# An adaLN transformer block on one core: when the inner rows' weights, the last operands, the slices' sums and the modulation weights are loaded and made

## Chip, core, metric

One core of a Trainium2 chip; everything is fp32. The metric is the device time of one execution in microseconds (us). A core has TensorE (PE, with its weight loads as PEld), VectorE (DVE), ScalarE (ACT), GpSimd (POOL) and SyncE (SP), whose queue issues nearly all DMAs of this kernel, in order.

## What is computed

For two sequences of 1024 tokens with D = 1024, one block with modulation from a vector c (six vectors per sequence: shift, scale and gate, for attention and for the FFN):

```
mod = silu(c) @ Wmod                      # sa, ca, ga, sf, cf, gf; |ga|, |gf| at least 0.25
h   = layernorm(x) * (1 + ca) + sa
q, k, v = clip(h @ Wqkv.T, -8, 8)         # q and k: layer norm over D, then 32 heads of 32
p   = softmax(q k^T / sqrt(32) + ALiBi + causal mask)
x1  = x + ga * ((p v) @ Wout.T)
h2  = layernorm(x1) * (1 + cf) + sf
x2  = x1 + gf * (ad * ((silu(ag * (h2 @ Wg.T)) * (au * (h2 @ Wu.T))) @ Wd.T))   # inner size 2752
```

## The kernel before

**Products.** Every large product is done in the Strassen-Winograd form with seven half-block products instead of eight (`seven`; the products are called P1, P2, U2, P5, U3, P53, U6). Its operands are sums and differences of quarters. For weights these sums are made on the chip and stored to device memory: `out_weights` for Wout, `down_weights` for Wd. `down_weights` works in 20 slices of 512 rows by two times 128 columns; a slice is four loads (L1211), four POOL subtractions (L1212 to L1215) and, a step later, four stores (L1218), in a pool with two buffers (tile `wdr`).

**Stages.** First come the modulation vectors, of which a first part is done ahead and the rest (`mod_product`, L618) is spread between the projection's products by `late`; `AHEAD` says how many loads (tile `wm`, pool `wmr`) run ahead of them. Then `projections` makes q, k, v of batch 0 and then of batch 1 (parts q, k, v by blocks of 256 tokens). From v of batch 0 on, attention runs beside it: `together` interleaves two generators, `attention` and `dense_work`, by `share`, which says how many us of dense work go with so many of attention. `dense_work` is the rest of batch 0's projection, batch 1's projection with the slices of `down_weights` as `side` work, and then `output` (Wout, gate, residual, second layer norm, turning rows) for the four blocks of batch 0 and the first two of batch 1.

`attention` goes by groups (batch, half of the queries, four heads) and by key blocks of 128: `scores` (products, exp on ACT at L1084, on the diagonal a causal mask by POOL's affine_select, L1088), `weigh` (product with V, and the sums of p for the softmax by DVE and POOL, L1116), `settle` (sums across partitions, stored; after the last head group of a half, `reciprocals` stores 1/sum as `rec`). A group's q, k and v (`chunk`: cq, ck, cv) are loaded when the second group before it ends.

`operand(b, j)` makes the seven operands of an output block: four loads of `rb` (the reciprocals spread over partitions, L1246), four of `ao` (L1260), four muls (L1261), four sums (L1262 to L1266); A21 and A22 have two buffers. `output` loads x (`xr`, L1289), reads the banks (L1293 to L1305), stores x1 (L1310) and puts layer norm and turning on a list.

After attention come the inner rows: 2752 is 5 x 512 + 192, and the last 192 rows of Wg and Wu are done apart by `rest_rows` with three weight tiles `restw`, made by `rest_weights` (a memset on POOL, L1365, and four loads, L1370). They are interleaved with the last two output blocks (1,2) and (1,3) and with the making of the FFN's operands (`second_batch`). `h2` of finished blocks is fetched again (tiles `hl`). Then comes the FFN.

**Order.** From the start of attention PE's order is the order in which the program writes its instructions. The order on the other engines is a scheduler's, within the data dependencies and explicit ties (`behind(a, b)`: a not before b). A pool that is opened where another has been closed takes its memory, and its tiles wait for the last users there.

What follows attention before the change:

```python
fetch(0, 0, nc.scalar)
rest_w = rest_weights(rest_pool, nc.scalar)     # loads on ACT's queue
fetch(1, 0, nc.scalar)
made = {(1, NJ // 2): operand(1, NJ // 2, opools[1])}
fetch(0, 1)
with_turns(rows((0, 0), (1, 0)))
fetch(1, 1)
...                                             # between(): rows (0, 1), second(0), rows (1, 1)
together(between(), output(1, range(NJ // 2, NJ), *out_args, made, 3), lambda a: 0.6 * OUT_US / 2 * a / 20.6)
```

Of the kernel before, what the change touches and what calls it, by code (L numbers as in the profile page):

```python
# [12 lines left out]
FP = mybir.dt.float32  # L13
# [5 lines left out]
P = 128  # L19
# [461 lines left out]
def kernel(  # L481
# [19 lines left out]
    nc = tc.nc  # L501
# [49 lines left out]
    NJ = NT // 2  # L551
# [111 lines left out]
    with tc.tile_pool(name="prep", bufs=1) as prep, tc.tile_pool(  # L663
        name="wmod", bufs=2 * KC
# [43 lines left out]
    def behind(ins, first):  # L708

        tc.add_manual_dep(  # L710
            ins.ins, first.ins.name,
            mybir.DependencyInfo(mybir.DependencyClass.NoSync, mybir.DependencyReason.DATA),
            reason="behind",
        )

    last_exp = [None]

    def normalize(tiles, outs, small, nm):

# [308 lines left out]
    def attention(pools, adders, banks):  # L1028
# [22 lines left out]
        def scores(b, qb, k, jb):  # L1051
            qc, kc, _ = chunks[b, qb, k]
            y0 = max(qb * QB, jb * P)
            end = (qb + 1) * QB
            n = end - y0
            span = SPAN.get(k, QB)
            out_ = {}
            first = None

            for half in (1, 0):  # L1060
                sp = scp.tile([P, 2, QB], FP, tag=f"sc{half}", name=f"sc_{b}_{k}_{qb}_{jb}_{half}")
                p = prp.tile(
                    [P, 2, QB], FP, tag="p" if jb else f"p0{half}", name=f"p_{b}_{k}_{qb}_{jb}_{half}",
                    bufs=None if jb else 2,
                )
                for g in range(2):
                    r0 = (2 * half + g) * HD
                    ins = matmul(
                        sp[:, g, 0:n], kc[r0 : r0 + HD, ts(jb, P)], qc[r0 : r0 + HD, ds(y0 - qb * QB, n)],
                        start=True, stop=True,  # L1070
                    )
                    if first is None:
                        first = ins
                    else:
                        behind(ins, first)
                out_[half] = (sp, p)
            for half in range(2):
                sp, p = out_[half]
                for g in range(2):
                    h_ = 4 * k + 2 * half + g  # L1080
                    for y in range(y0 // span * span, end, span):
                        lo, hi = max(y, y0) - y0, y + span - y0
                        d = jb - y // P + {128: 7, 256: 6, 512: 4}[span]
                        last_exp[0] = nc.scalar.activation(  # L1084
                            p[:, g, lo:hi], sp[:, g, lo:hi], AF.Exp, bias=kw[:, d, h_ : h_ + 1]
                        )
                if jb * P >= qb * QB:
                    nc.gpsimd.affine_select(  # L1088
                        out=p[:, :, 0:P], in_=p[:, :, 0:P], pattern=[[0, 2], [1, P]],
                        compare_op=ALU.is_ge, fill=0.0, base=0, channel_multiplier=-1,  # L1090
                    )
            return [out_[half][1] for half in range(2)]
# [110 lines left out]
    def down_weights(i, pool):  # L1203


        s, c_ = i // 4, i % 4
        w = pool.tile([P, 5, 2, P], FP, tag="wdr", name=f"wdr_{i}")
        rows_ = wd_t[ds(s * 4 * P, 4 * P), :].rearrange("(j p) e -> p j e", p=P)
        for kh in range(2):
            for n in range(2):  # L1210
                nc.sync.dma_start(w[:, 2 * kh + n], rows_[:, 2 * kh : 2 * kh + 2, ds(n * HALF + c_ * P, P)])  # L1211
        nc.gpsimd.tensor_sub(w[:, 0], w[:, 1], w[:, 0])  # L1212
        nc.gpsimd.tensor_sub(w[:, 4], w[:, 3], w[:, 0])
        nc.gpsimd.tensor_sub(w[:, 1], w[:, 3], w[:, 1])
        nc.gpsimd.tensor_sub(w[:, 2], w[:, 2], w[:, 4])  # L1215
        yield
        for o, r in (("T1", 0), ("T2", 4), ("T3", 1), ("T4", 2)):
            nc.sync.dma_start(wd_dram[o][:, s, :, ts(c_, P)], w[:, r])  # L1218
        yield
# [18 lines left out]
        rows_ = wd_t[0 : NSB * 4 * P, :].rearrange("(s m l p) e -> m l p s e", m=2, l=2, p=P)  # L1238
        return rows_[kh, l][:, :, ds(n * HALF + c * 256, 256)]

    def operand(b, j, ap_):

        qb, y0 = 2 * j * P // QB, 2 * j * P % QB
        rb = ap_.tile([P, KC, 2 * P], FP, tag="rb", name=f"rb_{b}_{j}")
        for g in range(4):
            nc.sync.dma_start(  # L1246
                rb[ts(g, HD)],
                rec_dram[b][qb].rearrange("(k g) q -> g k q", g=4)[g][:, ds(y0, 2 * P)].partition_broadcast(HD),
            )
        a = {  # L1250
            q: ap_.tile(
                [P, KC // 2, P], FP, tag=q, name=f"ao{q}_{b}_{j}",
                bufs=2 if q in ("A21", "A22") else None,
            )
            for q in ("A11", "A12", "A21", "A22", "S1", "S2", "S4")
        }
        for m, kh, q, eng in (
            (0, 0, "A11", nc.vector), (0, 1, "A12", nc.gpsimd), (1, 1, "A22", nc.vector), (1, 0, "A21", nc.gpsimd),
        ):
            nc.sync.dma_start(a[q], ao_dram[b][qb][:, ds(kh * 4, 4), ds(y0 + m * P, P)])  # L1260
            eng.tensor_mul(a[q], a[q], rb[:, ds(kh * 4, 4), ts(m, P)])  # L1261
        nc.vector.tensor_add(a["S1"], a["A21"], a["A22"])  # L1262
        nc.vector.tensor_sub(a["S2"], a["S1"], a["A11"])
        a["S3"] = a["A21"]
        nc.gpsimd.tensor_sub(a["S3"], a["A11"], a["A21"])
        nc.gpsimd.tensor_sub(a["S4"], a["A12"], a["S2"])  # L1266
        return a
# [3 lines left out]
    def output(b, js, pools, banks, bt, todo, keep, made={}, q0=1):  # L1271
# [9 lines left out]
        for j in js:  # L1281
# [9 lines left out]
            part_t = {}  # L1291

            def read(q, bank):  # L1293
                if q in ("P1", "U2", "P5"):
                    part_t[q] = partp.tile([P, 512], FP, tag=q, name=f"o{q}_{b}_{j}")
                    nc.scalar.copy(part_t[q], bank)
                    return
                m, n = QUAD[q]
                yg = partp.tile([P, 512], FP, tag=f"yg{n}", name=f"yg_{q}_{b}_{j}")
                if q == "U6":  # L1300
                    nc.vector.tensor_mul(yg, ga[:, ts(n, HALF)], bank)
                else:
                    nc.vector.tensor_add(yg, part_t[MATE[q]], bank)
                    nc.gpsimd.tensor_mul(yg, yg, ga[:, ts(n, HALF)])
                nc.gpsimd.tensor_add(xs[m][:, ts(n, HALF)], xs[m][:, ts(n, HALF)], yg)  # L1305

# [114 lines left out]
    three = [bankp.tile([P, 512], FP, tag=f"bank{i}", name=f"bank{i}") for i in range(3)]  # L1421
    with ExitStack() as st:
        five = st.enter_context(tc.tile_pool(name="five", bufs=1, space=PSUM))
        wmr = st.enter_context(tc.tile_pool(name="wmr", bufs=4))
        mrw = st.enter_context(tc.tile_pool(name="mrw", bufs=1))
        wosp = st.enter_context(tc.tile_pool(name="wos", bufs=1))
        nxp = st.enter_context(tc.tile_pool(name="next", bufs=1))
# [4 lines left out]
        banks = Banks(three[0:2], three[2:3] + more[2:5])  # L1432
        sums = {g: more[g - 1] for g in range(1, NMOD // 2)}
        pieces = [(g, k, n0) for k in range(KC) for g in sums for n0 in (0, 2)]
        AHEAD = 3
        loaded = []
        left = list(range(len(pieces)))

# [57 lines left out]
    def dense_work():  # L1496
        yield from dense0
        with tc.tile_pool(name="wdsum", bufs=2) as dwp:
            steps = itertools.chain.from_iterable(down_weights(i, dwp) for i in range(4 * NSB))

            def side(n, e):

                at = 7 * n + e - 24
                if at >= 0 and at % 3 != 2:
                    next(steps, None)

            yield from projections(1, qpools, banks, 1, side=side)
            for _ in steps:
                pass
        early.close()  # L1510
        hbp = right["hb"] = ost.enter_context(tc.tile_pool(name="hb", bufs=1))
        wop = ost.enter_context(tc.tile_pool(name="wo", bufs=1))
        gap_, tkp, partp, osm, aop = [
            ost.enter_context(tc.tile_pool(name=n, bufs=k))
            for n, k in (("oga", 1), ("tok", 4), ("opart", 1), ("osmall", 2), ("ao", 1))
        ]
        opools = (gap_, aop, tkp, partp, hbp, osm)
        made = {(0, 0): operand(0, 0, opools[1])}
        bt = weights_b(wop, wout_t, "o", wt_dram[3])
        out_args.extend((opools, banks, bt, Todo(banks), keep))  # L1520
        yield from output(0, range(NJ), *out_args, made)
        yield from output(1, range(NJ // 2), *out_args)


# [13 lines left out]
    pair_st = ctx.enter_context(ExitStack())  # L1538
    rest_st = ctx.enter_context(ExitStack())
    pair_pool = right["rest"] = pair_st.enter_context(tc.tile_pool(name="pair", bufs=1, side="right"))  # L1540
    rest_pool = rest_st.enter_context(tc.tile_pool(name="rest", bufs=1, side="right"))
    rps = rest_st.enter_context(tc.tile_pool(name="rest_ps", bufs=4, space=PSUM))

# [15 lines left out]
        together(rows_, todo.run(len(todo.list), True), lambda a: 0.16 * (a - 9.0))  # L1559

    fetch(0, 0, nc.scalar)
    rest_w = rest_weights(rest_pool, nc.scalar)
    fetch(1, 0, nc.scalar)
    made = {(1, NJ // 2): operand(1, NJ // 2, opools[1])}
    fetch(0, 1)
    with_turns(rows((0, 0), (1, 0)))
    fetch(1, 1)
# [477 lines left out]
```

## Time and profile before

| | |
|---|---|
| time, median of 3 runs | 2912.99 us (2908.82 to 2913.18) |
| the profiled execution: time, span | 2906.93 us, 2905.2 us |
| busy: PE, DVE, POOL, ACT | 2723.2, 1448.4, 1294.0, 685.7 us |
| mean granted PE clock | 0.976 |
| DMA | 579 MB, mean 199 GB/s |
| batch 0's projection alone | to about 350 us |
| attention beside dense work | to 1394 us |
| inner rows and the last two output blocks | 1394 to about 1557 us |
| FFN | from there to the end |

The profile is one execution, the times of its rows are on its own scale. PE is busy for 94% of the span, so what can be read from it are the stretches in which PE is empty or its granted clock (PEclk, a share of full speed) is under 1, and what ended each wait. In a window's row come its bounds, its length, and then the busy time of each engine with the number of instructions; in a wait's row the waiting engine, tile and line, then what it waited for, the us in total, the number of times and the longest; in a group's row the busy us and mean ns of one, and then the idle time of the engine just before them.

### The profile page before, as it was taken

The numbers are of one execution on the slowest core, as the hardware profiler recorded it, in microseconds if no ns is written. First come the engines' busy times: TensorE is split into PE (matmuls) and PEld (weight loads), VectorE is DVE, ScalarE is ACT, GpSimd is POOL, SyncE is SP. The second block draws the span as 40 slices with busy tenths as digits, with TensorE's granted clock in tenths as the row PEclk, the third lists the DMA queues.
The fourth block names the chain that finished last, engine by engine and source line by source line (L and its number), as shares of the span: only waits on it lengthen the run. The fifth ranks groups of instructions, "written<-read, shape, count | busy, mean of one in ns | idle before, by whom it ended". The sixth has DMA issues, their size and how long they took to land. (4 is left out here: it accounts for less than half of the span.)

```text
span 2905.2 us, 29905 instructions
## 1 busy us (share of the span) xinstructions
PE 2723.2 (94%) x10271; PEld 1336.5 (46%) x10271; DVE 1448.4 (50%) x2285; ACT 685.7 (24%) x1523; POOL 1294.0 (45%) x1270
## 2 busy tenths in 40 slices
PE   6999898999999898988799999999999998999998
PEld 2444333333333232222565444444444446888776
DVE  5765522566643456666464353453535346444442
ACT  1322232344444456555021011010101100000000
POOL 3311146523454665656357455464744541222343
PEclk9999999999999899999899999999999999999999
DMA  9877797563461555432777667585766659555542
GB/s 341 301 254 282 295 312 223 174 217 114 173 178 62 210 171 150 147 107 86 222 234 252 217 213 244 169 278 167 263 199 195 233 165 289 158 152 145 157 145 81
DMA packets 377573, 579.14 MB, mean 199 GB/s; under 512 B 21590, under 2 KB 278712, under 8 KB 366276
## 3 DMA queue, kind: packets, MB, share of 16 engines
q1 hardware_dynamic: 359768, 554.54, 58.8%
q10 hardware_dynamic: 17644, 22.59, 2.5%
q8 instruction: 84, 1.38, 0.2%
q14 instruction: 77, 0.63, 0.1%
HBM read 411.89 MB, written 165.17 MB: 199 GB/s over the span
## 5 line engine op out<-in xcount | busy, mean ns | idle before, releaser
L1084 ACT ACTIVATE p<-sc,kw 128x128 f32<-128x128 f32 (+3 forms) x1024 | 421.7, 513 | 382.5 <-PE sc L762 365.4
L762 PE MATMUL bank<-wT,a 128*128 128x512 f32 x768 | 360.0, 612 | 14.0 <-DVE raw L983 7.1
L1116 POOL TENSOR_TENSOR p<-p,p 128x1024 f32<-128x1024 f32 (+3 forms) x128 | 259.3, 2026 | 243.6 <-PE av L762 211.5
L1116 DVE TENSOR_TENSOR p<-p,p 128x1024 f32<-128x1024 f32 (+3 forms) x192 | 243.8, 1280 | 190.4 <-POOL p L1088 132.8
L762 PE MATMUL bank<-wB,a 128*128 128x512 f32 x576 | 266.0, 606 | 2.1 <-DVE raw L981 1.3
L762 PE MATMUL sc<-cq,ck 32*128 32x512 f32 (+3 forms) x1536 | 193.5, 543 | 53.0 <-ACT p L1084 52.7
L762 PEld LDWEIGHTS bank<-wT,a 128*128 128x128 f32 x768 | 142.6, 195 | 192.7 <-issue 174.6
L1088 POOL TENSOR_SCALAR_AFFINE_SELECT p<-p 128x256 f32<-128x256 f32 x256 | 139.2, 560 | 125.9 <-ACT p L1084 123.3
L762 PE MATMUL av<-p,cv 128*32 128x512 f32 (+3 forms) x1536 | 173.9, 514 | 16.6 <-POOL p L1088 16.6
L762 PEld LDWEIGHTS bank<-wB,a 128*128 128x128 f32 x576 | 105.1, 191 | 149.5 <-issue 128.8
L762 PEld LDWEIGHTS sc<-cq,ck 32*128 32x128 f32 x1536 | 64.9, 187 | 190.3 <-ACT p L1084 101.6
L1817 PE MATMUL gy<-bt,sig 128*128 128x512 f32 x280 | 132.5, 596 | 10.8 <-DMA bt<-bop_B 6.2
L1817 PE MATMUL gx<-bt,sig 128*128 128x512 f32 x280 | 131.6, 592 | 0.0
L1817 PE MATMUL uy<-bt,siu 128*128 128x512 f32 x280 | 131.6, 592 | 0.0
L1817 PE MATMUL ux<-bt,siu 128*128 128x512 f32 x280 | 131.6, 592 | 0.0
L762 PEld LDWEIGHTS av<-p,cv 128*32 128x32 f32 x1536 | 34.4, 110 | 139.1 <-issue 85.3
L1817 PEld LDWEIGHTS gy<-bt,sig 128*128 128x128 f32 x280 | 52.4, 190 | 81.1 <-issue 71.5
L1817 PEld LDWEIGHTS ux<-bt,siu 128*128 128x128 f32 x280 | 53.2, 190 | 66.9 <-issue 64.3
L1817 PEld LDWEIGHTS gx<-bt,sig 128*128 128x128 f32 x280 | 53.2, 190 | 66.9 <-issue 66.6
L1817 PEld LDWEIGHTS uy<-bt,siu 128*128 128x128 f32 x280 | 53.2, 190 | 66.9 <-issue 66.2
L762 PE MATMUL rest<-hl,restw 128*128 128x256 f32 x288 | 67.7, 394 | 15.7 <-DMA x<-xr 15.7
L1817 PE MATMUL gx<-bt,wgS 128*128 128x512 f32 x160 | 75.2, 592 | 0.0
(416 smaller groups left out, 4481.2 us busy)
## 6 DMA issues: line engine op xcount, KB each, us to landing
bt<-bop_T SPq DMA_DIRECT2D x140, 512.0 KB
bt<-bop_B SPq DMA_DIRECT2D x99, 512.0 KB
a<-hop SPq DMA_DIRECT2D x20, 1792.0 KB
wm<-in_L_wmod_dram SPq DMA_DIRECT2D x48, 512.0 KB
wB<-in_L_attn_Wqkv_dram SPq DMA_DIRECT2D x21, 1024.0 KB
aq_S<-act_S SPq DMA_DIRECT2D x16, 1280.0 KB
qk<-qs SPq DMA_DIRECT2D x16, 1024.0 KB
act_S<-asS SPq DMA_DIRECT2D x30, 512.0 KB
```

The costliest lines, as they stand in the source:

```text
L762: return in_order(nc.tensor.matmul(*args, **kw_))
L1084: last_exp[0] = nc.scalar.activation(p[:, g, lo:hi], sp[:, g, lo:hi], AF.Exp, bias=kw[:, d, h_ : h_ + 1])
L1088: nc.gpsimd.affine_select(out=p[:, :, 0:P], in_=p[:, :, 0:P], pattern=[[0, 2], [1, P]], compare_op=ALU.is_ge, fill=0.0, base=0, channel_mu ...
L1116: adders[b](half, jb).tensor_add(dst, dst, ps[half][:, :, 0:n])
L1817: nc.tensor.matmul(ps.rearrange("p (j t) -> p j t", j=NJ), ins[mat][qa][:, c2, :], bt[:, :, c2, :], start=(q in ("P1", "P2", "P5") and c2 ...
```

## The change

- `down_weights` has three steps instead of two: loads; sums; stores. The first sum of a slice is tied behind the last causal mask written so far (`last_mask`). `side` takes a step at each of its calls from call 24 on, where it took two of three; 20 slices are 60 steps where they were 40.
- The inner rows' weights get a pool of their own (`restw`) beside the output stage's pools, and are loaded on SP's queue after the output blocks of batch 0 are written, instead of on ACT's queue after attention.
- Operands (1,2) and (1,3) are both made right after attention, ahead of the inner rows; (1,2) has its own pool `wide`. In `operand`, A22 has one buffer instead of two.
- In `output`, the gated values `yg` are written over P's copies (U6 over P5's) instead of into tiles of their own; x rows have three buffers instead of four, the layer norm's small tiles one instead of two.
- The modulation weights have six buffers instead of four and run five ahead of their products instead of three.

```diff
@@ -714,6 +714,7 @@
         )
 
     last_exp = [None]
+    last_mask = [None]
 
     def normalize(tiles, outs, small, nm):
 
@@ -1085,7 +1086,7 @@
                             p[:, g, lo:hi], sp[:, g, lo:hi], AF.Exp, bias=kw[:, d, h_ : h_ + 1]
                         )
                 if jb * P >= qb * QB:
-                    nc.gpsimd.affine_select(
+                    last_mask[0] = nc.gpsimd.affine_select(
                         out=p[:, :, 0:P], in_=p[:, :, 0:P], pattern=[[0, 2], [1, P]],
                         compare_op=ALU.is_ge, fill=0.0, base=0, channel_multiplier=-1,
                     )
@@ -1203,13 +1204,15 @@
     def down_weights(i, pool):
 
 
+
         s, c_ = i // 4, i % 4
         w = pool.tile([P, 5, 2, P], FP, tag="wdr", name=f"wdr_{i}")
         rows_ = wd_t[ds(s * 4 * P, 4 * P), :].rearrange("(j p) e -> p j e", p=P)
         for kh in range(2):
             for n in range(2):
                 nc.sync.dma_start(w[:, 2 * kh + n], rows_[:, 2 * kh : 2 * kh + 2, ds(n * HALF + c_ * P, P)])
-        nc.gpsimd.tensor_sub(w[:, 0], w[:, 1], w[:, 0])
+        yield
+        behind(nc.gpsimd.tensor_sub(w[:, 0], w[:, 1], w[:, 0]), last_mask[0])
         nc.gpsimd.tensor_sub(w[:, 4], w[:, 3], w[:, 0])
         nc.gpsimd.tensor_sub(w[:, 1], w[:, 3], w[:, 1])
         nc.gpsimd.tensor_sub(w[:, 2], w[:, 2], w[:, 4])
@@ -1238,7 +1241,7 @@
         rows_ = wd_t[0 : NSB * 4 * P, :].rearrange("(s m l p) e -> m l p s e", m=2, l=2, p=P)
         return rows_[kh, l][:, :, ds(n * HALF + c * 256, 256)]
 
-    def operand(b, j, ap_):
+    def operand(b, j, ap_, own=None):
 
         qb, y0 = 2 * j * P // QB, 2 * j * P % QB
         rb = ap_.tile([P, KC, 2 * P], FP, tag="rb", name=f"rb_{b}_{j}")
@@ -1248,9 +1251,9 @@
                 rec_dram[b][qb].rearrange("(k g) q -> g k q", g=4)[g][:, ds(y0, 2 * P)].partition_broadcast(HD),
             )
         a = {
-            q: ap_.tile(
+            q: (ap_ if q == "S4" or own is None else own).tile(
                 [P, KC // 2, P], FP, tag=q, name=f"ao{q}_{b}_{j}",
-                bufs=2 if q in ("A21", "A22") else None,
+                bufs=2 if q == "A21" and own is None else None,
             )
             for q in ("A11", "A12", "A21", "A22", "S1", "S2", "S4")
         }
@@ -1296,11 +1299,12 @@
                     nc.scalar.copy(part_t[q], bank)
                     return
                 m, n = QUAD[q]
-                yg = partp.tile([P, 512], FP, tag=f"yg{n}", name=f"yg_{q}_{b}_{j}")
+
+                yg = part_t[MATE.get(q, "P5")]
                 if q == "U6":
                     nc.vector.tensor_mul(yg, ga[:, ts(n, HALF)], bank)
                 else:
-                    nc.vector.tensor_add(yg, part_t[MATE[q]], bank)
+                    nc.vector.tensor_add(yg, yg, bank)
                     nc.gpsimd.tensor_mul(yg, yg, ga[:, ts(n, HALF)])
                 nc.gpsimd.tensor_add(xs[m][:, ts(n, HALF)], xs[m][:, ts(n, HALF)], yg)
 
@@ -1421,7 +1425,7 @@
     three = [bankp.tile([P, 512], FP, tag=f"bank{i}", name=f"bank{i}") for i in range(3)]
     with ExitStack() as st:
         five = st.enter_context(tc.tile_pool(name="five", bufs=1, space=PSUM))
-        wmr = st.enter_context(tc.tile_pool(name="wmr", bufs=4))
+        wmr = st.enter_context(tc.tile_pool(name="wmr", bufs=6))
         mrw = st.enter_context(tc.tile_pool(name="mrw", bufs=1))
         wosp = st.enter_context(tc.tile_pool(name="wos", bufs=1))
         nxp = st.enter_context(tc.tile_pool(name="next", bufs=1))
@@ -1432,7 +1436,7 @@
         banks = Banks(three[0:2], three[2:3] + more[2:5])
         sums = {g: more[g - 1] for g in range(1, NMOD // 2)}
         pieces = [(g, k, n0) for k in range(KC) for g in sums for n0 in (0, 2)]
-        AHEAD = 3
+        AHEAD = 5
         loaded = []
         left = list(range(len(pieces)))
 
@@ -1500,8 +1504,7 @@
 
             def side(n, e):
 
-                at = 7 * n + e - 24
-                if at >= 0 and at % 3 != 2:
+                if 7 * n + e >= 24:
                     next(steps, None)
 
             yield from projections(1, qpools, banks, 1, side=side)
@@ -1512,13 +1515,15 @@
         wop = ost.enter_context(tc.tile_pool(name="wo", bufs=1))
         gap_, tkp, partp, osm, aop = [
             ost.enter_context(tc.tile_pool(name=n, bufs=k))
-            for n, k in (("oga", 1), ("tok", 4), ("opart", 1), ("osmall", 2), ("ao", 1))
+            for n, k in (("oga", 1), ("tok", 3), ("opart", 1), ("osmall", 1), ("ao", 1))
         ]
         opools = (gap_, aop, tkp, partp, hbp, osm)
         made = {(0, 0): operand(0, 0, opools[1])}
         bt = weights_b(wop, wout_t, "o", wt_dram[3])
+        rwp = ost.enter_context(tc.tile_pool(name="restw", bufs=1))
         out_args.extend((opools, banks, bt, Todo(banks), keep))
         yield from output(0, range(NJ), *out_args, made)
+        right["w"] = rest_weights(rwp, nc.sync)
         yield from output(1, range(NJ // 2), *out_args)
 
 
@@ -1538,6 +1543,7 @@
     pair_st = ctx.enter_context(ExitStack())
     rest_st = ctx.enter_context(ExitStack())
     pair_pool = right["rest"] = pair_st.enter_context(tc.tile_pool(name="pair", bufs=1, side="right"))
+    wide = rest_st.enter_context(tc.tile_pool(name="wide", bufs=1, side="right"))
     rest_pool = rest_st.enter_context(tc.tile_pool(name="rest", bufs=1, side="right"))
     rps = rest_st.enter_context(tc.tile_pool(name="rest_ps", bufs=4, space=PSUM))
 
@@ -1559,9 +1565,10 @@
         together(rows_, todo.run(len(todo.list), True), lambda a: 0.16 * (a - 9.0))
 
     fetch(0, 0, nc.scalar)
-    rest_w = rest_weights(rest_pool, nc.scalar)
+    rest_w = right["w"]
     fetch(1, 0, nc.scalar)
-    made = {(1, NJ // 2): operand(1, NJ // 2, opools[1])}
+    made = {(1, NJ // 2): operand(1, NJ // 2, opools[1], wide)}
+    made[1, NJ // 2 + 1] = operand(1, NJ // 2 + 1, opools[1])
     fetch(0, 1)
     with_turns(rows((0, 0), (1, 0)))
     fetch(1, 1)
```

## The prediction

> **What bounds the kernel now.** I read the busy shares first: TensorE (PE) works 2723 of 2905 us, so only its empty stretches are to be had, 182 us in all, and what a lower clock costs after them. Then I cut the span into stretches and read PE busy and granted clock in each (columns: stretch, PE, weight loads, DVE, ACT, POOL, PEclk, DMA share, GB/s):
>
> ```profile
> 300.00:350.00 50.00, 42.38 (x137) 17.73 (x138) 19.96 (x48) 11.40 (x27) 2.53 (x2) 0.97 0.84 300
> 450.00:530.00 80.00, 62.18 (x273) 23.53 (x272) 28.80 (x56) 23.16 (x51) 54.69 (x81) 0.87 0.70 211
> 530.00:600.00 70.00, 66.88 (x332) 26.22 (x335) 34.50 (x72) 33.70 (x97) 22.45 (x27) 1.00 0.60 204
> 832.00:865.00 33.00, 29.09 (x132) 10.31 (x128) 15.65 (x16) 13.29 (x27) 19.19 (x16) 0.95 0.64 155
> 940.00:1000.00 60.00, 48.86 (x240) 14.71 (x238) 25.89 (x22) 28.14 (x77) 36.71 (x32) 0.86 0.62 225
> 1394.00:1432.00 38.00, 18.54 (x77) 15.40 (x77) 19.49 (x35) 3.20 (x6) 13.20 (x9) 0.76 0.73 184
> ```
>
> Two stretches that the edits touch are thin: 450–530 (17.8 us empty) and 1394–1432 (19.5 us empty). A gap costs more than its length: after it the clock rows show 0.5 for pieces of 3.4 to 17 us, and half of the matmul time in such a piece is lost. I add that loss: 8.1 us in 450–530, 2.4 us in 1394–1432, 6.0 us in 940–1000.
>
> The waits of 450–530, when down_weights' sums run:
>
> ```profile
> DVE p L1116 <- POOL p L1088: 38.0, 6, 10.6
> PEld av L762 <- POOL p L1088: 17.1, 9, 5.3
> POOL wdr L1212 <- DMA wdr<-in_L_ffn_Wd_dram: 15.6, 5, 3.7
> PE av L762 <- POOL p L1088: 12.6, 5, 4.7
> ```
>
> POOL sits in front of its own queue waiting for a slice's load; the causal masks (L1088) stand behind, and the products with V and the DVE adds behind the masks.
>
> The waits of 1394–1432, where attention has ended:
>
> ```profile
> PE rest L762 <- DMA x<-xr: 15.7, 1, 15.7
> POOL aoA L1261 <- DMA rb<-rec: 12.3, 1, 12.3
> POOL restw L1365 <- DMA rec<-rc: 6.6, 1, 6.6
> ```
>
> PE waits 15.7 us for the first inner-row product: its weights are only asked for at 1401.5 to 1404.8, since their pool lies where attention's buffers were. The release that the profile names (a store of x) is the last event, not the cause. The hl operands were asked for before 1393 and are there.
>
> **Slices' sums (−22, +5).** 80 POOL subtractions stand in 355–527 us: 80 × 0.73 = 58 us (61 with the long ones), plus 64 us of waits for loads:
>
> ```profile
>   POOL wdr L1212: 41.1, 8
>   POOL wdr L1213: 22.9, 11
> ```
>
> The work stays; it goes behind masks, a step after the load. In the changed order the sums reach from about 577 to 932 us, most of them in the long ends of the head groups. There POOL has room: from 600 to 940 it is busy 147 of 340 us, and one wait alone holds 116 us of what is free:
>
> ```profile
> L1116 POOL TENSOR_TENSOR p<-p,p 128x1024 f32<-128x1024 f32 x28 | 81.5, 2912 | 128.1 <-PE av L762 116.1 <-ACT p L1084 10.7
> ```
>
> In 450–530 the loss is 17.8 + 8.1 = 25.9 us. What stays I take from the stretch behind it, which has the same work without sums: 3.1 us in 70, so 3.5 in 80. Gain 22.4. In return 61 us of sums lie among masks and adds. The cost lies between 0 (all in the 193 us that POOL has free) and 15: a row of sums in 450–530 costs PE 22.4 / 62 us (35.8 work and 26.4 wait there) = 0.36 us each, and two thirds of 61 at that rate are 15. I take 5, as the order puts most sums where POOL waits for the next group's products. Stores of the slices move along on SP; each waits there for its sums, with later chunk loads of attention behind it, which were asked for a group (about 48 us) ahead. Three steps instead of two leave the load a whole turn to land, so the DMA wait goes.
>
> A rule speaks against this part. The trace's POOL add of 128x1024 takes 2912 ns in this stretch, against 1.8 us where no DVE add runs beside it. The Trainium skill, "SBUF — State Buffer", section "Who interferes with whom", holds that VectorE and GpSimd share a port pair as an exclusive lock for a whole instruction, also against DVE operations with two SBUF inputs. By that, as an estimate, each of the 80 sums could stand behind one DVE add (1.23 us alone), 98 us more; and the gain of this part would be gone. Before, sums took 756 ns in 450–530 beside busy DVE, hardly over their 0.72.
>
> **Modulation weights (−5).** With five loads ahead of their products instead of three:
>
> ```profile
> 306.09 1.05 PE L618 MATMUL more<-wm,sc 128*32 128x512 f32 x4 [3.38 <-DMA wm<-in_L_wmod_dram]
> 341.80 1.88 PE L618 MATMUL more<-wm,sc 128*32 128x512 f32 x4 [3.39 <-DMA wm<-in_L_wmod_dram]
> ```
>
> The last load was issued at 334.1, behind a store on SP; issued two products earlier it is there. I take one gap with its half-clock piece, 3.4 + 1.7 = 5.1; the bounds are 0 and 9.3, the whole of 300–350's loss.
>
> **Inner rows' weights and the two operands (−19).** Before, PE is empty from 1394.4 to 1410.1, then works 28 us on inner rows, waits 3.8 us at 1430 on turned rows, and reaches the output product at 1443.5. With weights loaded during the output stage, inner rows start at once. The memset (L1365) leaves POOL too; it held the last x add (L1305, now at 1402.5) behind a wait for a DMA, so the last LN moves up by some 7 us and the 1430 gap closes. Gain: 15.7 + 3.8 + 2.4 of clock = 21.9, less about 3, since 28 us of rows must now cover rc → rec → rb → muls → S-sums (rb loads were issued at 1401.3 to 1410, with 12.3 us of POOL waiting). If rb lands at 1413 and five dependent sums of 1.3 to 1.8 follow, that is 1421, just before the rows end at 1423. So −19; bounds −6 (chain late by 13, had the second operand's four loads and muls gone between) and −22. Operand (1,3) is made right after, off PE's path.
>
> **Around 840 and 947 (−4, +7).** The first output operand's loads ran at 810–835 and its muls waited on POOL 12 us; PE lost 3.9 us at 832–865. In the changed order these loads (2 MB) and the inner rows' weights (1.5 MB) come after the last slice stores, ahead of the weights of the output product on SP. That product already waits:
>
> ```profile
> 947.41 2.04 PE L762 MATMUL bank<-wB_o,aoA 128*128 128x512 f32 x2 [3.91 <-DMA wB_o<-in_L_attn_Wout_dram]
> ```
>
> wB_o was issued at 941.5 and took 5.9 us. 3.5 MB at the 300 GB/s that the 300–350 stretch moved take 12 us; by its place in SP's order I put wB_o at about 947, the product at 954: +7, with bounds 0 (loads done during the last projection) and +12.
>
> **Smaller buffers in the output stage (+3).** A22 has one buffer instead of two, xr three instead of four, LN's small tiles one instead of two, and yg is written over P's copies. Between a block's last read of A22 and the next block's first use lie at least 21 us (1164 to 1185.5), against load 3 + mul 1 + sums 1.3. PE lost 58 us idle in 1000–1394, mostly on scores; +3 within 0 and +8.
>
> **Sum.** −22.4 + 5 − 5.1 − 19 − 4 + 7 + 3 = −35.5. From the profiled execution's 2906.9 us that is 2871; this execution lies 6.1 us (0.2%) below the median of the three runs, so against 2913 I say 2878. Everything at its good end is −22 − 9 − 22 − 4 = −57, at its bad end −22 − 0 − 6 − 0 + 15 + 12 + 8 = +7.
>
> **Rivals.** *Given back at 947 and in the tail:* the 12 us of the queue, and the tail gains 6 instead of 19: −35.5 + 5 + 13 = −17.5, 2895. For it: SP is one ordered queue and 3.5 MB are put ahead of weights that PE already waits for; against it: the rows' weights are small beside 12 us of rows.
>
> *Slower, through POOL:* sums among masks, stretched by DVE adds as the 128x1024 adds are (2.9 / 1.8 = 1.6), make 98 us; if each goes to PE at 0.6 us (they stand straight behind masks, and the next mask behind them) that is 59 instead of 5: +18, 2931. It decides from 0.66 us of PE loss per us of sum (40.5 / 61) unstretched, 0.41 stretched. For it: DVE waits for masks 52 us in 600–940 already. Against it: POOL's free time there is three times the sums.
>
> *Nothing happens:* a stall at 450–530 that comes from scores and projections' loads, not sums, stays; with the tail at −6 and the costs as above the change is 0 ± 6, 2913.
>
> **Chances.** Forecast 0.60 (2863–2890), given back 0.20, nothing 0.08, slower 0.12. The range 2861 to 2906 takes in the forecast with its good end and the first rival with worse costs. A measurement here tells about 0.2% (6 us) from no change; faster by more than that: 0.81, within it 0.07, slower 0.12.
>
> **What would show it.** Right: 450–530 PE busy near 76 at clock 1.0; no wait of wdr sums for DMA; inner rows starting by 1396 on the old scale; no wait at 342. Wrong in a step: POOL p L1088 as the releaser of PE in 600–940 with more than 15 us; PE's wait for wB_o over 15 us; aoA waiting for rb after the rows end; A22 or xr naming PE's waits in the output stage. A median over 2906 makes the whole wrong.

## The result and the profile after

The changed kernel takes 2905.3 us (median of 20 runs, 2896.0 to 2914.5) against 2910.3 of the kernel before (20 runs): ratio 0.9986, with a 95% interval of 0.9978 to 0.9994. It is faster by 0.14%, some 5 us, where 35 were forecast. Its profiled execution took 2896.0 us (span 2894.3), 9 under the median, so I read the places and not the total from it.

The stretches of before, as they stand now (the last one is the same work, on the new scale; 865–940 holds the first output product). A line of the program has a number here that is one to seven higher than before: L763 is L762 of before.

```profile
300.00:350.00 50.00, 48.88 (x161) 23.19 (x160) 30.87 (x65) 12.04 (x27) 5.66 (x4) 1.00 0.79 286
450.00:530.00 80.00, 76.28 (x405) 29.17 (x407) 40.33 (x77) 32.54 (x71) 27.46 (x40) 1.00 0.29 93
832.00:865.00 33.00, 32.19 (x149) 11.45 (x150) 12.13 (x12) 14.05 (x27) 19.88 (x21) 1.00 0.54 169
865.00:940.00 75.00, 55.76 (x251) 18.65 (x250) 23.32 (x24) 24.98 (x49) 43.91 (x37) 0.89 0.74 227
1392.00:1430.00 38.00, 34.44 (x144) 26.69 (x143) 25.52 (x48) 4.72 (x9) 16.62 (x11) 0.96 0.75 224
```

The stalls of these stretches are gone or small: 450–530 has 76 us of PE work at full clock (62 at 0.87 before), the inner rows 34 of 38 (18.5 at 0.76 before). The new hole is at 865–940. To see where the time went I follow one event of the trace through all kernels: ACT's copies of a P product (two for each projection or output block). Before, the last copy of batch 1's projection is at 925 us and after at 880: a lead of 45 us. The first copy of output block (0,0) is at 956 and 924: 32 left. The last copy of block (1,1), at the end of attention, is at 1384 and 1382: 2 left. Then the first of block (1,2) is at 1447 and 1428: 19 again. The last copy of all, of block (1,3), is at 1499 and 1482: 17. The first product of the FFN is at 1557 and 1546, and the spans end at 2905 and 2894: 11 at both. So the gain was made where it was meant to be, and given back in three steps: 13 us at the first output product, 31 us in an output stage that takes 458 us from its first to its last copy and took 427, and 9 us between the first copy of block (1,2) and the FFN.

The waits of the changed kernel from 905 to 1394, PE first, then DVE and POOL:

```profile
PE sc L763 <- ACT p L1085: 46.8, 41, 3.7
PE bank L763 <- DVE aoS L1266: 17.7, 1, 17.7
PE av L763 <- POOL p L1089: 17.2, 7, 5.1
PE bank L763 <- DVE h2t L869: 15.2, 2, 8.6
...
DVE aoA L1264 <- DMA aoA<-ao: 25.5, 4, 11.7
...
POOL aoA L1264 <- DMA rb<-rec: 19.1, 2, 10.1
```

In the same stage before (925 to 1394, PE, then DVE):

```profile
PE sc L762 <- ACT p L1084: 45.2, 41, 3.8
PE bank L762 <- DVE h2t L868: 4.5, 1, 4.5
PE av L762 <- POOL p L1088: 4.0, 4, 2.1
...
DVE aoA L1261 <- DMA aoA<-ao: 3.7, 1, 3.7
```

PE's waits for masks and for turned rows (h2t) have grown by 24 us in all, DVE's for ao by 22, and POOL had none for rb; the waits for attention's exponentials (sc) are as they were. One of the waits, followed back through the rows of SP, DVE and PE:

```profile
992.09 0.32 SPq L1047 DMA_DIRECT2D cq<-qk  x1
998.84 0.33 SPq L1292 DMA_DIRECT2D xr<-_attn_hidden_states_dram  x1
...
1001.23 0.45 SPq L1263 DMA_DIRECT2D aoA<-ao  x1
...
1011.02 0.71 DVE L1264 TENSOR_TENSOR aoA<-aoA,rb 128x512 f32<-128x512 f32 x1 [10.95 <-DMA aoA<-ao]
1011.65 1.36 DVE L869 TENSOR_SCALAR h2t<-bank,modt 128x128 f32<-128x128 f32 x4
...
1013.06 1.94 PE L763 MATMUL bank<-p,ones 128*32 128x512 f32 x8 [6.65 <-DVE h2t L869]
```

SP stands still from 992.5 to 998.8 in front of a load of x, whose buffer is not free (DVE's normalisation still reads it); the ao load behind it goes out at 1001.2; DVE stands in front of the multiplication by it until 1011.0; the turned rows behind that multiplication free a bank of PSUM (where PE's products go) only then, and PE's sums for the softmax wait 6.65 us for the bank. That is the theory to test: *the late operand and the small buffers* (A). The rival (B): the output stage goes at the pace of attention's exponentials and masks, and gives back any lead that it is handed.

### The profile page after: what moved, and what is told of

Same layout as the page of the kernel before. It is cut to its first block, busy times and chain, and to the rows that moved or that the text cites. A ratio compares the mean times of both kernels' runs of the same rounds, so it can differ in the third digit from the quotient of the medians.

```text
span 2894.3 us, 29930 instructions
## 1 busy us (share of the span) xinstructions
PE 2702.2 (93%) x10271; PEld 1330.2 (46%) x10271; DVE 1453.0 (50%) x2285; ACT 685.2 (24%) x1523; POOL 1296.8 (45%) x1270
## 4 chain that ended last, share of the span: by engine, by line
PE 43%; DMA 4%; DVE 3%; issue 3%; POOL 3%; ACT 1%; SPq 0%; POOLq 0%; DVEq 0%; ACTq 0%
PE gx L1824 7%; PE ux L1824 7%; PE dx L1949 7%; PE gy L1824 6%; PE uy L1824 6%; PE dy L1949 5%; PE bank L763 1%; DMA bt<-bop_B 1%; DMA bop_T<-inner_T 1%; PE sc L763 1%; ACT p L1085 1%; DMA wuA<-in_L_ffn_Wu_dram 1%; PE rest L763 0%; PE av L763 0%; DVE asS L1778 0%
## 5 line engine op out<-in xcount | busy, mean ns | idle before, releaser
L763 PE MATMUL bank<-wT,a 128*128 128x512 f32 x768 | 353.6, 603 | 12.0 <-DVE wT L832 6.8
L763 PE MATMUL bank<-wB,a 128*128 128x512 f32 x576 | 262.5, 601 | 1.2 <-DVE raw L982 0.6
L763 PE MATMUL sc<-cq,ck 32*128 32x512 f32 (+3 forms) x1536 | 194.5, 548 | 56.4 <-ACT p L1085 56.1
L763 PEld LDWEIGHTS bank<-wT,a 128*128 128x128 f32 x768 | 140.0, 192 | 186.2 <-issue 168.9
L763 PE MATMUL av<-p,cv 128*32 128x512 f32 (+3 forms) x1536 | 173.2, 514 | 17.2 <-POOL p L1089 17.2
L763 PEld LDWEIGHTS bank<-wB,a 128*128 128x128 f32 x576 | 104.5, 190 | 145.0 <-issue 123.6
L763 PEld LDWEIGHTS sc<-cq,ck 32*128 32x128 f32 x1536 | 64.5, 186 | 193.6 <-ACT p L1085 103.0
L1824 PE MATMUL gy<-bt,sig 128*128 128x512 f32 x280 | 132.4, 595 | 10.7 <-DMA bt<-bop_B 5.7
L763 PEld LDWEIGHTS av<-p,cv 128*32 128x32 f32 x1536 | 34.0, 110 | 138.7 <-issue 80.7
L763 PE MATMUL bank<-wB_o,aoA 128*128 128x512 f32 x128 | 68.3, 667 | 18.7 <-DVE aoS L1266 17.7
L1824 PE MATMUL ux<-bt,wuS 128*128 128x512 f32 x160 | 75.2, 592 | 0.0
```

The lines of the kernel that those rows point to most:

```text
L763: return in_order(nc.tensor.matmul(*args, **kw_))
L1824: nc.tensor.matmul(ps.rearrange("p (j t) -> p j t", j=NJ), ins[mat][qa][:, c2, :], bt[:, :, c2, :], start=(q in ("P1", "P2", "P5") and c2 ...
```

## Experiments

All times are medians; the kernel before, on the same chips, took 2910 to 2912 us (e1 to e8 ran on one chip, e9 to e12 on another). The stage is the time between the first and last P copies of the output blocks (0,0) to (1,1).

| kernel | us | ratio to before (95%) | output stage |
|---|---|---|---|
| before | 2910.3 | | 427 |
| the changed kernel | 2905.3 | 0.9986 (0.9978 to 0.9994) | 458 |
| e1 slices alone | 2891.2 | 0.9933 (0.9920 to 0.9945) | 426 |
| e2 small buffers alone | 2947.0 | 1.0134 (1.0119 to 1.0149) | 458 |
| e3 changed, operand early | 2912.9 | 1.0008 (0.9997 to 1.0020) | 457 |
| e4 changed, slices undone | 2929.0 | 1.0070 (1.0057 to 1.0083) | 461 |
| e5 A22 one | 2924.7 | 1.0052 (1.0037 to 1.0066) | 440 |
| e6 x rows three | 2908.7 | 0.9997 (0.9988 to 1.0007) | 419 |
| e7 gated values, small tiles | 2907.6 | 0.9991 (0.9981 to 1.0001) | 424 |
| e8 slices early, weights ahead | 2870.6 | 0.9864 (0.9849 to 0.9880) | 427 |
| e9 A22 one, x rows three | 2940.4 | 1.0110 (1.0090 to 1.0129) | 458 |
| e10 slices, weights ahead | 2874.0 | 0.9878 (0.9858 to 0.9898) | 426 |
| e11 changed, A22 two | 2883.0 | 0.9908 (0.9890 to 0.9925) | 421 |
| e12 e8, other order of pools | 2866.2 | 0.9849 (0.9833 to 0.9864) | 424 |

**e1, the slices alone.** On the kernel before, only this (and `last_mask` kept as in the change):

```diff
+        yield
+        behind(nc.gpsimd.tensor_sub(w[:, 0], w[:, 1], w[:, 0]), last_mask[0])
...
-                at = 7 * n + e - 24
-                if at >= 0 and at % 3 != 2:
+                if 7 * n + e >= 24:
```

> Only the slices' sums behind masks in three steps, on the kernel before. In the changed kernel PE reached the first output product 31 us sooner than before and had lost nearly all of it by the end of attention. Theory A (late operand and small buffers): here PE comes to the output stage about 25 to 35 us ahead, waits 8 to 18 us for operand (0,0), which is tied behind the last slice, and keeps the rest, since the buffers are the old ones: 12 to 20 us faster than before. Theory B (the output stage runs at the pace of attention's exponentials and masks and gives back whatever lead it is handed): within 5 us of before.

20.5 us faster, and the output stage keeps its length: what is won ahead of it is not given back. Theory B falls here. PE's waits from 870 to 1400 (those for exponentials, 46.9 us, and for the first inner row, 16.1, left out):

```profile
...
PE bank L763 <- DMA wB_o<-in_L_attn_Wout_dram: 11.2, 1, 11.2
PE bank L763 <- DVE h2t L869: 4.5, 1, 4.5
PE av L763 <- POOL p L1089: 4.0, 4, 2.1
```

The price at the first output product is there (11.2 against 3.9 before), the waits for turned rows and masks are those of before.

**e2, the small buffers alone.**

```diff
-                bufs=2 if q in ("A21", "A22") else None,
+                bufs=2 if q == "A21" else None,
...
+                yg = part_t[MATE.get(q, "P5")]
...
+            for n, k in (("oga", 1), ("tok", 3), ("opart", 1), ("osmall", 1), ("ao", 1))
```

> Only the smaller buffers of the output stage (A22 one, x rows three, small tiles one, gated values over P's copies), on the kernel before. Theory A: 15 to 30 us slower than before, all of it in the output stage, with DVE waiting at the operand's multiplication for its ao load, POOL for rb, and PE for DVE's turned rows and POOL's masks behind them. Theory B: within 5 us of before. My prediction's step had +3 (0 to 8).

35.4 us slower, more than theory A's 15 to 30; 31 of them are the output stage. The waits of the changed kernel come back in a kernel that has nothing else of it (940 to 1420, DVE, POOL, PE):

```profile
DVE aoA L1261 <- DMA aoA<-ao: 21.2, 3, 11.3
...
POOL aoA L1261 <- DMA rb<-rec: 30.4, 3, 12.5
...
PE av L762 <- POOL p L1088: 15.8, 7, 5.1
PE bank L762 <- DMA wB_o<-in_L_attn_Wout_dram: 14.9, 1, 14.9
PE bank L762 <- DVE h2t L868: 14.6, 2, 7.4
```

The wait for wB_o is one that theory A did not expect here: the first output product is late (14.9 us against 3.9 before) though no slice is late and no inner rows' weights stand in front. The first copy of block (0,0) comes at 964.5 instead of 956.5. The first load of operand (0,0), in before and in this kernel:

```profile
810.67 0.33 SPq L1246 DMA_DIRECT2D rb<-rec  x1
```

```profile
934.76 0.33 SPq L1246 DMA_DIRECT2D rb<-rec  x1
```

SP stands 9.6 us in front of the second one, until DVE is done with rows of the last projection (`raw`). So with all four cuts the operand seems to lie in memory that the projection holds until then. None of e5, e6, e7 and e9, which have one or two of the cuts, shows this wait (4.0 to 4.3 us for wB_o); that it is the place in memory was not tried.

**e3, the operand early.** The changed kernel with slices begun at call 8 and the `restw` pool opened before the output stage's other small pools:

```diff
-                if 7 * n + e >= 24:
+                if 7 * n + e >= 8:
...
+        rwp = ost.enter_context(tc.tile_pool(name="restw", bufs=1))
         gap_, tkp, partp, osm, aop = [
```

> The changed kernel with the slices begun at call 8 instead of 24, so that they end sooner, and with the inner rows' weights' pool opened ahead of the operand's, so that the operand's memory is the slices' and its loads stand ahead of the inner rows' weights. Theory A: PE's 17.7 us wait for the first output operand is gone, the lead of some 44 us at 925 us reaches the output stage; the small buffers still cost their 25 to 30: 10 to 20 us faster than the changed kernel. Theory B: the same as the changed kernel within 4 us.

A miss in its total, 7.6 us slower than the changed kernel where A said 10 to 20 faster, for a reason outside both theories. The 17.7 us wait is gone (4.5 remain) and the kernel is 9 us ahead of the changed one up to the last output block (1473 against 1482) and the FFN's first product (1537 against 1546). Then, a few products into the FFN:

```profile
PE gx L1824 <- POOL sig L1689: 20.3, 1, 20.3
```

POOL's first sums of gate weights (L1677) wait 6.0 us for PE's inner rows in this kernel: moved to another place, the inner rows' weights seem to lie where those sums are to go. That the pools' order does this was not tried apart from the earlier slices.

**e4, the slices undone in the changed kernel**, i.e. the inverse of the edit of e1.

> The changed kernel with the slices' sums as before (two steps, no mask tie). Theory A: the stall at 450 to 530 is back (20 to 25 us), the wait for the first output operand is short (under 5), the small buffers cost 25 to 30, the tail gains 17 and the modulation weights 5: 5 to 15 us slower than the changed kernel. Theory B: the same as the changed kernel.

23.6 us slower than the changed kernel, more than A's 5 to 15, with the stall at 450–530 back: the slices are worth about the same here as alone. A's short wait for the first output operand (under 5) is a miss:

```profile
PE bank L763 <- DMA wB_o<-in_L_attn_Wout_dram: 14.9, 1, 14.9
```

The slices are early again and the product is late all the same, as in e2: the operand's loads go out from 926.7 on.

**e5, e6, e7: which buffer.** Each is one part of e2 on the kernel before: A22 in one buffer; x rows (`tok`) in three; the gated values over P's copies with `osmall` in one.

> Only A22 in one buffer, on the kernel before; all four small-buffer edits together cost 35 us. Theory A1 (A22): its load cannot be issued until the block before has used A22, DVE's multiplication stands in order in front of turned rows and adds: 15 us or more slower than before, with DVE waiting over 15 us for aoA from ao. Theory A2 (x rows): within 5 us of before.

> Only the x rows in three buffers instead of four, on the kernel before. Theory A1 (A22): within 5 us of before. Theory A2 (x rows): the load of the next block's second x tile stands on SP until the x store of the block before has landed, and holds the rb and ao loads and chunk loads behind it: 15 us or more slower, with POOL waiting over 15 us for rb.

> Only the gated values over P's copies and the layer norm's small tiles in one buffer, on the kernel before. Both theories on A22 and x rows: within 5 us of before. A third (A3): P's copy of the next block waits for the gated add, and PE for ACT's copies: 10 us or more slower, with ACT's copies and PE's banks as the waits.

A22 costs 15 us (14.7), the other two nothing. DVE's waits for ao in e5 were 11.7 us, less than the 15 that its theory asked for, and the three parts do not add up to the 35 us of all.

**e8, slices early and weights ahead, none of the rest.**

> The kernel before with the slices' sums behind masks, begun at call 8 instead of 24, and the modulation weights five ahead; nothing else of the change. With the slices alone PE waited 11.2 us for the output weights, against 3.9 before, since operand (0,0)'s loads follow the last slice on SP. If the last slice sets that wait, it falls to about 4 and its half clock goes: 7 to 9 us gained, and 5 more from the modulation weights: 2876 to 2880 against 2891 of the slices alone. If the wait comes from SP's other traffic, only the modulation weights show: 2885 to 2888.

2870.6, better than either expectation: PE's wait for wB_o is 4.1 us again (11.2 in e1; 11.9 in e10, which has the same modulation weights and begins the slices at call 24), so it was the slices' end that set it. The remaining gain comes from the modulation weights (below).

**e9, A22 and the x rows together** (both edits of e5 and e6).

> A22 in one buffer and the x rows in three, on the kernel before, gated values and small tiles as they were. A22 alone cost 15 us, the x rows alone nothing, the other two nothing, all four 35. If A22 and the x rows act together (the late x load on SP holds back the late A22 load, and the multiplications wait in order behind both): 30 to 37 us slower than before. If the gated values over P's copies are what adds to A22: 13 to 18 us slower.

30 us slower than before, and the stage is the 458 us of the changed kernel. The pair is the loss of the stage: the x rows' shortage, free by itself, doubles what A22's single buffer costs. What e2 has beyond it is the late first product. The trace shows the chain of the changed kernel again (SP in front of xr, then DVE 11.8 us in front of the multiplication, then PE 7.5 us for the bank). That SP's order is the link between the two was read, not tried.

**e10, slices and weights ahead, as in the change** (call 24).

> The kernel before with the two parts that need no memory of the output stage, as the change has them: the slices' sums behind masks in three steps from call 24 on, and the modulation weights five ahead. Slices alone gave 2891. If the parts add as measured so far (the modulation weights are worth some 13 to 20 us of lead before the output stage, of which none is given back with the old buffers): 2872 to 2880, so the rest of the change (inner rows' weights early, small buffers, both operands) costs 25 to 35 us net. If the first operand's lateness eats the modulation weights' share: 2885 to 2891.

2874.0, as the first case had it. So the rest of the change costs 31 us net, give or take some 6 us (the six executions range from 2870.7 to 2886.9).

**e11, the changed kernel with A22 in two buffers.** The third tile of the inner rows' weights is loaded after attention to pay for it, and S2 of operand (1,2) goes to the old pool:

```diff
-                bufs=2 if q == "A21" and own is None else None,
+                bufs=2 if q in ("A21", "A22") and own is None else None,
...
-    rest_w = right["w"]
+    rest_w = right["w"] + [rest_third(rest_pool, nc.scalar)]
```

> The changed kernel with A22 in two buffers again; its memory is had by loading the third of the three weight tiles of the inner rows after attention as before, and by making S2 of operand (1,2) in the old pool. If A22's single buffer is what turns the x rows' shortage into a loss: the output stage is back to some 430 us from 458, 18 to 30 us faster than the changed kernel, 2877 to 2887. If the x rows' three buffers do harm of their own in this order: within 8 us of the changed kernel.

22 us faster than the changed kernel, and the stage is 421 us, 37 less, with x rows still in three buffers. So most of what the change lost hangs on one tile of 2 KB per partition: with it the change is worth 27 us, not 5. The third weight tile's late load was tried only together with it; PE waits 12.4 us for an inner row after attention here, which takes part of the stage's gain back, and the first output product is still late (15.5 us).

**e12, e8 with attention's pools in the order rs, prob, chunk** instead of chunk, prob, rs.

> The kernel of slices early and modulation weights ahead (2870.6), with attention's pools opened in another order, so that the inner rows' weights lie where attention's q, k, v chunks were, which are free some 10 us before its end, and not where the reciprocals are stored from; no memory is taken from the output stage. If PE's 14.9 us at the start of the inner rows are the wait for that memory: 5 to 12 us faster, the fetched rows of h2 then setting the start. If h2's rows, which now lie where p was, come as late as the weights did: the same within 4 us.

2866.2 us, the lowest of all: 44 us under before. Its wait at the first inner row, in place of e8's 14.9:

```profile
PE rest L763 <- DVE ve_f L734: 9.2, 1, 9.2
```

The gain over e8 is 4.4 us, between the two expectations (5 to 12, and within 4), and the intervals of the two ratios touch. So the wait did get 5.7 us shorter, but the time does not decide; what sets the remaining 9 us was not tried.

## Why the prediction was wrong, step by step

**Slices' sums: right.** −17.4 was said, −20.5 measured alone (e1), of which the later first product has already been taken off: at the last copy of the projection e1 leads by 23 us (902 against 925). The sums took 722 ns in the median, and PE did not wait for masks once from 530 to 900:

```profile
L1117 POOL TENSOR_TENSOR p<-p,p 128x1024 f32<-128x1024 f32 x28 | 80.7, 2882 | 99.9 <-PE av L763 88.1 <-ACT p L1085 10.7
...
L1215 POOL TENSOR_TENSOR wdr<-wdr 128x256 f32<-128x256 f32 x20 | 16.3, 813 | 5.3 <-DMA wdr<-in_L_ffn_Wd_dram 5.3
```

All 80 sums took 60.7 us there, against 58 at 0.73 each. The rule of the Trainium skill ("SBUF — State Buffer", "Who interferes with whom"), by which each sum could stand behind one of DVE's adds, was put at 98 us more; under 3 were seen on POOL. No run here separates the rule from the place of the sums, which lie where POOL waits for the next group. One reading beside it was wrong: 1.8 us is what a POOL add of 128x768 takes at its shortest; of 128x1024 the shortest take 2.35 us. So the stretch by DVE's adds, from which the rival "slower, through POOL" was reckoned, is 2.91 / 2.35 = 1.24 and not 1.6.

**Modulation weights: right in sign, too small.** −5 was said (bounds 0 and 9.3); e10 against e1 gives −17 by the medians, of two chips, and −12 by the traces (last copy at 1469 against 1481), and in e4 the lead over before is 13 us at the 20th copy (336 against 349) and 6 us at 577. The wait shrank as said (6.8 to 2.5 us), but I left out that the scheduler would put the products in other places when their loads come earlier. The group of these products, 160 to 350 us, before and after:

```profile
L618 PE MATMUL more<-wm,sc 128*32 128x512 f32 x128 | 28.7, 617 | 6.8 <-DMA wm<-in_L_wmod_dram 6.8
```

```profile
L618 PE MATMUL more<-wm,sc 128*32 128x512 f32 x128 | 19.8, 601 | 2.5 <-DMA wm<-in_L_wmod_dram 2.5
```

The same 128 products take 8.9 us less of PE, and the wait 4.3 us less: 13 us, the lead of e4. Before, 19 of their 24 clusters were single groups of four products; after, 4 of 13.

**The tail: right at its head, half of it kept.** −19 was said; from the last copy of block (1,1) to the first of (1,2) it is 46 us and was 63: −18. The 15.7 us wait is gone. But the wait for turned rows at 1430 did not close as forecast: 3.6 us of such waits stand in 1392–1430, and one of 3.9 us behind the last output block, with a granted clock of some 0.5 for 3 us after it:

```profile
1486.12 1.11 PE L766 MATMUL bank<-ident,xn 128*128 128x128 f32 x4 [3.88 <-DVE h2t L869]
```

From the last copy of block (1,3) to the FFN's first product it is 64 us and was 58. From the end of attention to the FFN the gain is 9 us, not 18.

**840: right; 947: the price too small, the wrong tile, and a cause left out.** The stretch 832–865 gained 3.1 us, 4 were said. For the first output product +7 was said, with 12 as the bound, and wB_o as the tile that is late. The wait is 17.7 us instead of 3.9, and it is for the operand: its rb loads go out at 892.9 to 899.9 and its ao loads at 901 to 907, ahead of wB_o at 907, and DVE's and POOL's multiplications and sums follow their landing. I counted the queue and left out the chain of arithmetic behind it, and that smaller buffers could move the operand itself. Two causes are each enough for a long wait: the slices' late end (11.2 us in e1, 11.9 in e10, against 4.1 in e8) and the four cuts of buffers together (14.9 in e2 and e4, where no slice is late). The changed kernel has both, so its 17.7 us do not split into shares; e3, with earlier slices and another order of pools, has 4.5.

**Small buffers: the step that failed.** +3 was said, with 8 as the bound; 35 measured (e2), 31 of them in the output stage, as in the changed kernel. My argument was that 21 us lie between A22's last use and the next block's first, against 3 + 1 + 1.3 of work. That is A22's own chain. A load can take longer than 3: in the rows from 992 on, the multiplication by an ao load begins 9.8 us after its issue. And the chain says nothing of who stands behind it. In those rows SP, DVE and PE each stand in front of an instruction whose buffer or load is late, and what comes next in their order waits too: ao behind x, the turned rows behind the multiplication. POOL waits 19.1 us for rb in the same stage, and PE 17.2 us for POOL's masks instead of 4.0. I named that question for the slices and did not ask it for the buffers. I also gave the four cuts one price from A22's chain, where two of them act together (e5, e6, e9). And the 58 us of PE's idle time beside it are those of 940–1394; 1000–1394 has 47.

The single runs overlap (the first product's wait is in e1 and in e2), so they do not add up to one sum. The two traces do: the lead at the end of the projection, the loss at the first output product, the loss in the output stage, the gain at the head of the tail, the loss up to the FFN: 45.2 − 12.8 − 30.7 + 17.8 − 8.8 = 10.7. The medians differ by 5, since the profiled execution after is the fastest of its 20. The rival "given back at 947 and in the tail" had both its places right (13 us, and 9 us from the tail where it said 6) and missed the largest, the output stage.

## What to carry to other kernels

When a change buys memory for an early load by cutting buffers elsewhere, price the cut by what is queued behind the instruction that now waits, on every queue that it passes (the DMA queue and each engine), and not by the slack of its own chain. See too what else moves when pools shrink: here the first operand's loads went from 811 to 935 us. Cuts that are free one at a time can cost together, so try them as the set that will be used. And look for memory that is free early before taking it from a stage that uses its buffers; e12 is a first try at that, with no memory taken from the output stage.

## What was not expected of the hardware

Four products with the modulation weights (tile wm) between other products took 1.05 us, as the row at 306.09 of before shows; 20 of them in a row took far less than five times that:

```profile
214.83 2.77 PE L618 MATMUL more<-wm,sc 128*32 128x512 f32 x20
```

That is 0.14 us each against 0.26, while the mean duration of one is 0.6 us in both kernels: in a row, more of them overlap.
